# Summing four quarters of channels before the bias product, two of the three sums as accumulating DMA transfers

## The chip, the cores and the metric

The kernel runs on one NeuronCore of a Trainium2 chip. The core has a matrix engine (TensorE, PE in the profile), a vector engine (DVE), an activation engine (ACT), a general engine (GpSimd, POOL) and SyncE (SP), which here only starts transfers. Each works through its own queue in order; semaphores hold an instruction back until what it needs is there. Sixteen DMA engines move data. The metric is the device time of one execution in microseconds (us), as the median of several runs. The profile belongs to one execution.

## The reference, cut to what matters

The network has four layers on a small image. The change touches layer 0, a deformable attention block, and in it only the position bias. For each of 16 combinations of batch and head there are 1024 queries and 64 sampled keys. The bias of every query-key pair comes from a small network with 128 hidden channels in both of its layers:

```python
pos = grid_q[:, :, None, :] - grid_kv[:, None, :, :]
bias = jnp.sign(pos) * jnp.log1p(jnp.abs(pos))
bias = jax.nn.relu(bias @ cpb_w1 + cpb_b1)      # 2 -> 128
bias = jax.nn.relu(bias @ cpb_w2 + cpb_b2)      # 128 -> 128
bias = (bias @ cpb_w3 + cpb_b3)                 # 128 -> 1
sim = jnp.einsum('bhid,bhjd->bhij', qh, kh) + bias
attn = jax.nn.softmax(sim, axis=-1)
```

With 16 x 1024 x 64 query-key pairs the second line with a `relu` is by far the largest product of the layer. The last product sums 128 channels with the weights `cpb_w3`.

## The kernel before

Layer 0 works through a list `quads` of (u, o, jj): 16 values of u (batch and head), 8 of o, 2 of jj, 256 in all. One such step handles four keys (keys 32 jj + 4 o to 32 jj + 4 o + 3 of head u) for all 1024 queries. Two steps with jj = 0 and 1 form a pair.

**First hidden layer** (`first_hidden`, L392). DVE makes four tiles of 128 channels x 1024 queries, one for each key, from a table in SBUF and a row in PSUM, always one step ahead of their use. There are four `h1` buffers of two keys each.

**Second hidden layer** (`second_hidden`, L414). The 128 output channels are cut into four quarters q of 32. For each q, TensorE multiplies 32 columns of the weights with each of the four keys' tiles. The results stand side by side in one accumulator `hp`: partitions 32 k to 32 k + 31 hold key k. Three accumulators rotate. ACT then adds the bias and applies the `relu` (L418), writing a tile `y` of 128 x 1024 into the pool `hid2`.

**Last product by signs.** The absolute value of `cpb_w3` has been multiplied into the second layer's weights and bias ahead of time (`last_weights`), so the last product only has to add channels with a sign of plus or minus one. Before that product, quarters 0 and 1 are summed, and quarters 2 and 3: the even quarter is multiplied by the product of the two signs (`flip`; on ACT at L425 for q = 0, on POOL at L422 for q = 2), then POOL adds the odd quarter (L426). What is left is two tiles for each step.

**The last product** (`last_product`, L441). A matrix `ends` with the odd quarters' signs in a block pattern sums the 32 rows of each key and puts the result into the right row of the accumulator `sim`. It runs once for a pair, with four products of 512 columns for each of the two sums.

**The order of the work** is written out by hand: the program order is the order in each queue of PE, ACT, DVE and POOL (`manual_schedule`). In a step the next step's first hidden layer is issued first, then this step's second one. The last product of a pair follows the second hidden layer of the next step (the jj = 0 step of the next pair). Behind each step come one piece of `after` (softmax and output of a finished head, `attend`, and at the end of a batch `projection`) and one piece of `front` (offsets and samples of the next channel tile, `offsets` and `sampled`). Loads of the tables `lb` go through SP's queue; no transfer is started by POOL.

After layer 0 come the block's own multi-layer perceptron and the three other layers, which the change leaves alone.

Of the kernel before, what the change touches and what calls it, by code (L numbers as in the profile page):

```python
# [11 lines left out]
F32 = mybir.dt.float32  # L12
AF = mybir.ActivationFunctionType
ALU = mybir.AluOpType
# [33 lines left out]
class Net:  # L48
# [50 lines left out]
    def layer0(self):  # L99


        nc, io = self.nc, self.io
        with ExitStack() as ctx:
            keep = self.pool(ctx, "l0")
            self.l0qkv = keep.tile([P, 3, CT, P], F32, tag="qkv", name="qkv")
            nc.scalar.dma_start(self.l0qkv, io["l0_qkv"])
            self.l0w2 = keep.tile([P, P], F32, tag="w2", name="w2")
            nc.scalar.dma_start(self.l0w2, io["cpb_w2"])
            ow = keep.tile([P, CT, C], F32, tag="ow", name="ow")
            nc.scalar.dma_start(ow, io["out_w"])  # L110
            self.s1 = self.bn(keep, "bn1")
            self.last_weights(keep)

            self.dram = ctx.enter_context(self.tc.tile_pool(name="l0_d", bufs=2, space=bass.MemoryType.DRAM))
            self.fpool = self.pool(ctx, "f", 2)
            self.fone = self.pool(ctx, "f1", 1)
            self.lpool = self.pool(ctx, "c_log", 2)
            self.tab = self.pool(ctx, "c_tab", 2)
            self.hid = self.pool(ctx, "c_hid", 4)
            self.hid2 = self.pool(ctx, "c_hid2", 11)  # L120
            self.soft = self.pool(ctx, "c_soft", 1)
            apool = self.pool(ctx, "c_att", 1)
            ps = self.ps_h = self.pool(ctx, "c_ps_h", 3, psum=True)

            self.bank = self.pool(ctx, "c_ps_t", 1, psum=True).tile([P, HF], F32, tag="bank", name="bank")
            ps_s = self.pool(ctx, "c_ps_s", 1, psum=True)

            engines = {getattr(mybir.EngineType, e) for e in ("PE", "Activation", "DVE", "Pool")}
            with self.tc.manual_schedule(engines=engines):
                pairs = [{} for _ in range(BP)]  # L130
                for _ in self.offsets(pairs[0], 0, ps):
                    pass
                front = [self.sampled(pairs[0], 0, ps)]
                after, sims, att = [], {}, None
                tables = {}
                quads = [(u, o, jj) for u in range(2 * BP) for o in range(8) for jj in range(2)]
                ready = self.first_hidden(*quads[0], pairs, tables)
                held = None
                for i, (u, o, jj) in enumerate(quads):
                    if o == 0 and jj == 0 and u % 2 == 0 and u // 2 + 1 < BP:  # L140
                        nxt = pairs[u // 2 + 1]
                        front += [self.offsets(nxt, u // 2 + 1, ps), self.sampled(nxt, u // 2 + 1, ps)]
                    h1 = ready
                    if i + 1 < len(quads):
                        if quads[i + 1][1:] == (7, 0) and u + 1 < 2 * BP:
                            self.advance(front, lambda: "logs" in pairs[(u + 1) // 2])
                        ready = self.first_hidden(*quads[i + 1], pairs, tables)
                    z = self.second_hidden(u, o, jj, h1)
                    if jj == 0:
                        if held is not None:  # L150
                            self.last_product(*held, sims, ps_s)
                            if held[1] == 7:
                                v = held[0]
                                if v % 8 == 0:
                                    self.advance(after, lambda: False)
                                    att = [
                                        apool.tile([P, N], F32, tag=f"att{t}", name=f"att{v}_{t}") for t in range(CT)
                                    ]
                                self.advance(front, lambda: "v" in pairs[v // 2])
                                after.append(self.attend(v, pairs[v // 2], sims.pop(v), att, ps))  # L160
                                if v % 8 == 7:
                                    after.append(self.projection(ps, att, ow, v // 8))
                        first = z
                    else:
                        held = (u, o, (first, z))
                    self.step(after)
                    self.step(front)
                self.last_product(*held, sims, ps_s)
                after.append(self.attend(u, pairs[u // 2], sims.pop(u), att, ps))
                self.advance(after, lambda: False)  # L170
                self.project(ps, att, ow, "out_b", B - 1)

    def last_weights(self, keep):

        nc = self.nc
        row = keep.tile([P, P], F32, tag="row", name="w3row")
        nc.scalar.dma_start(row, self.io["cpb_w3"].partition_broadcast(P))  # L180
        nc.vector.scalar_tensor_tensor(row, row, -1.0, row, ALU.mult, ALU.max)
        nc.vector.tensor_tensor(self.l0w2, self.l0w2, row, ALU.mult)
        w3 = self.colr("w3r", 4)
        self.magb = keep.tile([P, 4], F32, tag="magb", name="magb")
        nc.vector.scalar_tensor_tensor(self.magb, w3, -1.0, w3, ALU.mult, ALU.max)
        nc.vector.tensor_tensor(self.magb, self.magb, self.colr("b2r", 4), ALU.mult)
        sign = keep.tile([P, 4], F32, tag="sign", name="sign")
        nc.vector.tensor_scalar(sign, w3, 0.0, 2.0, ALU.is_ge, ALU.mult)
        nc.vector.tensor_scalar(sign, sign, -1.0, None, ALU.add)
        self.flip = keep.tile([P, 2], F32, tag="flip", name="flip")  # L190
        self.ends = keep.tile([P, 2, 60], F32, tag="ends", name="ends")
        nc.vector.memset(self.ends, 0.0)
        for p in range(2):
            nc.vector.tensor_tensor(
                self.flip[:, p : p + 1], sign[:, 2 * p : 2 * p + 1], sign[:, 2 * p + 1 : 2 * p + 2], ALU.mult
            )
            for k in range(4):
                rows = slice(32 * k, 32 * k + 32)
                nc.vector.tensor_copy(self.ends[rows, p, 28 + k : 29 + k], sign[rows, 2 * p + 1 : 2 * p + 2])

    @staticmethod
    def step(behind):
# [200 lines left out]
    def second_hidden(self, u, o, jj, h1):  # L403


        nc = self.nc
        got, before = [], None
        for q in range(4):
            hp = self.ps_h.tile([P, N], F32, tag="ps", name=f"hp_{u}_{o}{jj}{q}")
            for h in range(2):  # L410
                cut = slice(h * HF, (h + 1) * HF)
                for k in range(4):
                    rows = slice(32 * k, 32 * k + 32)
                    nc.tensor.matmul(  # L414
                        hp[rows, cut], lhsT=self.l0w2[:, 32 * q : 32 * q + 32], rhs=h1[k][:, cut], start=True, stop=True
                    )
            y = self.hid2.tile([P, N], F32, tag="h2", name=f"h2_{u}_{o}{jj}{q}")
            nc.scalar.activation(y, hp, AF.Relu, bias=self.magb[:, q : q + 1])  # L418
            if q % 2 == 0:
                before = y  # L420
                if q == 2:
                    nc.gpsimd.tensor_scalar(y, y, self.flip[:, 1:2], 1.0, ALU.mult, ALU.mult)  # L422
            else:
                if q == 1:
                    nc.scalar.activation(before, before, AF.Copy, scale=self.flip[:, 0:1])  # L425
                nc.gpsimd.tensor_tensor(y, y, before, ALU.add)  # L426
                got.append(y)
        return got

    def last_product(self, u, o, z, sims, ps_s):  # L430

# [2 lines left out]
        nc = self.nc  # L434
        if o == 0:
            sims[u] = ps_s.tile([P, HF], F32, tag="sim", name=f"sim{u}")
        for p in range(2):
            for h in range(2):
                for jj in range(2):
                    at = h * NJ + jj * 32  # L440
                    nc.tensor.matmul(  # L441
                        sims[u][at : at + 32, :],
                        lhsT=self.ends[:, p, 28 - 4 * o : 60 - 4 * o],
                        rhs=z[jj][p][:, h * HF : (h + 1) * HF],
                        start=(o == 0 and p == 0),
                        stop=False,
                    )

    def attend(self, u, m, sim, att, ps):
        nc = self.nc  # L450
# [701 lines left out]
```

## Time and profile before

| | us |
|---|---|
| median of 3 runs | 3705.47 (3703.88 to 3705.98) |
| span of the profiled execution | 3703.5 |
| layer 0's hidden matmuls, first to last start | 42.2 to 2186.3 |
| PE busy, of the span | 3610.2 (97%) |
| POOL, ACT busy, of the span | 1868.3 and 1860.3 (50% each) |
| POOL adds of quarters (L426), 512 | 1228.7 |
| sim matmuls (L441), 2048 recorded | 251.1 |

Two things help in reading it. A float32 matmul appears as two recorded instructions, so the 8 matmuls of one `last_product` are 16 in the trace. And an instruction's mean time is not its cost where several run beside each other: the matmuls of 32 columns work in groups of four, so the distance between groups is what counts. Idle time of an engine names who released it; on an engine that doesn't set the pace, that idle time costs nothing.

### The profile page before, as it was taken

How to read it: one execution, taken by the hardware profiler on the slowest of the kernel's cores; microseconds unless marked ns; L12 is line 12 of the kernel's file. 1: busy time of each engine (PE TensorE's matmuls, PEld its weight loads, DVE VectorE, ACT ScalarE, POOL GpSimd, SP SyncE). 2: the span in 40 equal slices, each digit the busy share in tenths (PEclk: the TensorE clock that was granted, in tenths of full speed). 3: DMA queues.
4: the chain of work that ended last, by engine and by line, in shares of the span. 5: the costliest groups of instructions: out<-in, count | busy, mean ns of one | idle time of the engine just before them, and what ended most of it. 6: DMA issues, size and time to landing. Idle time of an engine off the chain costs nothing.

```text
span 3703.5 us, 59657 instructions
## 1 busy us (share of the span) xinstructions
PE 3610.2 (97%) x26176; PEld 1282.8 (35%) x26176; DVE 2036.4 (55%) x2075; ACT 1860.3 (50%) x1873; POOL 1868.3 (50%) x1013
## 2 busy tenths in 40 slices
PE   5999999999999999999999989999989999999998
PEld 2232332332333332332333324444454333343333
DVE  5777667668667567668666640000052377522764
ACT  4766676776766576766667641100010266102661
POOL 3777777777776577777777750000001244012441
PEclk8999999999999999999999999999999999999999
DMA  3000000000000000000100021000000000000001
GB/s 91 16 18 18 17 21 13 20 18 20 13 18 18 14 18 16 17 18 20 34 14 22 15 91 46 0 0 0 0 4 1 35 1 1 16 0 1 1 1 47
DMA packets 28628, 68.37 MB, mean 18 GB/s; under 512 B 4416, under 2 KB 6080, under 8 KB 27072
## 3 DMA queue, kind: packets, MB, share of 16 engines
q1 hardware_dynamic: 27488, 62.34, 5.9%
q8 instruction: 209, 3.42, 0.4%
q10 hardware_dynamic: 864, 2.06, 0.2%
q14 instruction: 67, 0.55, 0.1%
HBM read 59.92 MB, written 4.46 MB: 17 GB/s over the span
## 4 chain that ended last, share of the span: by engine, by line
PE 88%; DVE 10%; DMA 1%; issue 1%; POOL 0%; ACT 0%; DVEq 0%; ACTq 0%; SPq 0%; POOLq 0%
PE hp L414 42%; PE m L545 6%; PE m L554 6%; PE s L882 6%; PE o L911 6%; PE sim L441 5%; DVE h L392 4%; PE qk0p L774 3%; PE pb L511 3%; PE qk1p L774 3%; PE vp L815 3%; DVE prod L245 2%; PE out_b L511 2%; DVE conv L258 1%; PE d L928 1%
## 5 line engine op out<-in xcount | busy, mean ns | idle before, releaser
L414 PE MATMUL hp<-h,w 128*32 128x512 f32 x16384 | 1822.2, 593 | 16.6 <-DVE h L392 15.0
L426 POOL TENSOR_TENSOR h<-h,h 128x1024 f32<-128x1024 f32 x512 | 1228.7, 2400 | 576.4 <-ACT h L425 555.0
L418 ACT ACTIVATE h<-hp,magb 128x1024 f32<-128x1024 f32 x1024 | 1139.0, 1112 | 659.0 <-PE hp L414 621.8
L392 DVE CUSTOM_DVE_ANT_1 h<-tx,bank 128x1024 f32<-128x1024 f32 x1024 | 1180.5, 1216 | 393.3 <-PE hp L414 386.2
L414 PEld LDWEIGHTS hp<-h,w 128*32 128x32 f32 x16384 | 530.1, 110 | 1246.5 <-issue 1196.4
L886 ACT ACTIVATE e<-s 128x1024 f32<-128x1024 f32 x256 | 258.6, 1023 | 152.8 <-PE s L882 152.7
L422 POOL TENSOR_SCALAR h<-h,flip 128x1024 f32<-128x1024 f32 x256 | 297.5, 1162 | 0.0
L425 ACT ACTIVATE h<-h,flip 128x1024 f32<-128x1024 f32 x256 | 291.0, 1137 | 0.0
L882 PE MATMUL s<-q,k 64*64 64x512 f32 x2048 | 259.9, 590 | 5.1 <-ACT e L886 3.4
L911 PE MATMUL o<-e,v 64*64 64x512 f32 x2048 | 260.8, 592 | 0.0
L441 PE MATMUL sim<-h,ends 128*32 128x512 f32 x2048 | 251.1, 594 | 2.9 <-POOL h L426 2.9
L585 POOL MEMSET l1ones<- 128x128 f32 x1 | 0.2, 204 | 483.8 <-PE m L554 483.8
L545 PE MATMUL m<-mx,w 128*128 128x512 f32 x512 | 220.5, 592 | 0.8 <-DVE x L515 0.8
L554 PE MATMUL m<-mh,w 128*128 128x512 f32 x512 | 220.4, 592 | 0.0
L549 ACT ACTIVATE mh<-m,cols 128x512 f32<-128x512 f32 x64 | 44.0, 687 | 336.5 <-PE m L545 336.5
L893 POOL TENSOR_TENSOR some<-some,e 128x1024 f32<-128x1024 f32 x64 | 151.2, 2363 | 82.6 <-ACT e L886 80.2
L562 DVE SCALAR_TENSOR_TENSOR x<-m,cols,x 128x512 f32<-128x512 f32 x16 | 12.0, 751 | 318.0 <-PE m L554 318.0
L891 POOL TENSOR_TENSOR some<-e,e 128x1024 f32<-128x1024 f32 x32 | 75.8, 2369 | 212.6 <-ACT q L920 139.2
L788 POOL TENSOR_TENSOR sq<-q 128x1024 f32<-128x1024 f32 x16 | 30.3, 1892 | 279.3 <-DVE q L782 279.3
L786 ACT ACTIVATE k<-qk1p,cols 128x512 f32<-128x512 f32 x32 | 22.0, 687 | 244.5 <-PE qk1p L774 244.5
L545 PEld LDWEIGHTS m<-mx,w 128*128 128x128 f32 x512 | 97.2, 190 | 123.6 <-issue 122.0
L554 PEld LDWEIGHTS m<-mh,w 128*128 128x128 f32 x512 | 97.3, 190 | 122.4 <-issue 122.4
(180 smaller groups left out, 2420.6 us busy)
## 6 DMA issues: line engine op xcount, KB each, us to landing
lb<-logs SPq DMA_DIRECT2D x64, 512.0 KB, 4.9
w<-in_mlp_w SPq DMA_DIRECT2D x8, 1024.0 KB, 12.1
qkv<-in_l_qkv SPq DMA_DIRECT2D x8, 768.0 KB, 6.4
x<-in_x SPq DMA_DIRECT2D x8, 512.0 KB, 8.1
out<-x SPq DMA_DIRECT2D x8, 512.0 KB, 2.6
proj<-in_l_proj SPq DMA_DIRECT2D x8, 256.0 KB, 5.9
l1w<-in_l_w SPq DMA_DIRECT2D x1, 1280.0 KB, 6.9
ow<-in_out_w ACTq DMA_DIRECT2D x1, 1024.0 KB, 12.2
```

The costliest lines, as they stand in the source:

```text
L392: self.nc.vector._custom_dve(TENSOR_ADD_SAT, out=h[:, k, :, :], in0=x[:, jj, 2 * r + k, :].unsqueeze(1).to_broadcast([P, H, W]), in1=y[:, ...
L414: nc.tensor.matmul(hp[rows, cut], lhsT=self.l0w2[:, 32 * q : 32 * q + 32], rhs=h1[k][:, cut], start=True, stop=True)
L418: nc.scalar.activation(y, hp, AF.Relu, bias=self.magb[:, q : q + 1])
L422: nc.gpsimd.tensor_scalar(y, y, self.flip[:, 1:2], 1.0, ALU.mult, ALU.mult)
L425: nc.scalar.activation(before, before, AF.Copy, scale=self.flip[:, 0:1])
L426: nc.gpsimd.tensor_tensor(y, y, before, ALU.add)
L441: nc.tensor.matmul(sims[u][at : at + 32, :], lhsT=self.ends[:, p, 28 - 4 * o : 60 - 4 * o], rhs=z[jj][p][:, h * HF : (h + 1) * HF], start= ...
L545: nc.tensor.matmul(acc, lhsT=w1[t][:, o * P : (o + 1) * P], rhs=xn[t], start=(t == 0), stop=(t == CT - 1))
L554: nc.tensor.matmul(acc, lhsT=w2[t // 4][:, t % 4, o * P : (o + 1) * P], rhs=hs[t], start=(t == 0), stop=(t == nh - 1),)
L882: nc.tensor.matmul(s[halves[c], par, :], lhsT=ks[p][rows, at : at + DH], rhs=qs[p][rows, cut], start=True, stop=True)
L886: nc.scalar.activation(e, s, AF.Exp)
L911: nc.tensor.matmul(o[halves[par], r, :], lhsT=v[rows, n, at : at + DH], rhs=e[rows, par, :], start=(n == 0), stop=(n == NB - 1),)
```

## The change

All four quarters are summed before the last product, so that one tile for each step is left and `last_product` runs four products for a pair instead of eight. Each of the first three quarters is multiplied by its sign times the sign of quarter 3. Quarter 0 is flipped by ACT, quarter 1 by ACT in jj = 0 steps and by POOL in jj = 1 steps, quarter 2 by POOL.

Of the three sums one stays an add on POOL (quarter 3 += quarter 2). The other two are transfers inside SBUF that add to their destination: quarter 1 += quarter 0 is started in the step itself, and quarter 3 += quarter 1 (`join`) in the following step, right after that step's own first transfer. Both go through POOL's queue.

The last product of a pair is issued one step later than before, after the second hidden layer of the next pair's jj = 1 step. The eleven buffers of `hid2` become 2, 3, 2 and 4 for the four quarters.

```diff
-            self.hid2 = self.pool(ctx, "c_hid2", 11)
+            self.hid2 = self.pool(ctx, "c_hid2", 1)
...
                     z = self.second_hidden(u, o, jj, h1)
                     if jj == 0:
+                        first = z
+                    else:
                         if held is not None:
                             self.last_product(*held, sims, ps_s)
...
-                        first = z
-                    else:
                         held = (u, o, (first, z))
...
+                self.join()
                 self.last_product(*held, sims, ps_s)
...
-            y = self.hid2.tile([P, N], F32, tag="h2", name=f"h2_{u}_{o}{jj}{q}")
+            y = self.hid2.tile([P, N], F32, tag=f"h2{q}", bufs=(2, 3, 2, 4)[q], name=f"h2_{u}_{o}{jj}{q}")
+            ys.append(y)
             nc.scalar.activation(y, hp, AF.Relu, bias=self.magb[:, q : q + 1])
-            if q % 2 == 0:
-                before = y
-                if q == 2:
+            if q == 1:
+                nc.scalar.activation(ys[0], ys[0], AF.Copy, scale=self.flip[:, 0:1])
+                if jj == 1:
                     nc.gpsimd.tensor_scalar(y, y, self.flip[:, 1:2], 1.0, ALU.mult, ALU.mult)
-            else:
-                if q == 1:
-                    nc.scalar.activation(before, before, AF.Copy, scale=self.flip[:, 0:1])
-                nc.gpsimd.tensor_tensor(y, y, before, ALU.add)
-                got.append(y)
-        return got
+                else:
+                    nc.scalar.activation(y, y, AF.Copy, scale=self.flip[:, 1:2])
+                nc.gpsimd.dma_start(y, ys[0], accum_op=ALU.add)
+                if self.join:
+                    self.join()
+            elif q == 2:
+                nc.gpsimd.tensor_scalar(y, y, self.flip[:, 2:3], 1.0, ALU.mult, ALU.mult)
+            elif q == 3:
+                nc.gpsimd.tensor_tensor(y, y, ys[2], ALU.add)
+        self.join = lambda: nc.gpsimd.dma_start(ys[3], ys[1], accum_op=ALU.add)
+        return ys[3]
...
-        for p in range(2):
-            for h in range(2):
-                for jj in range(2):
-                    at = h * NJ + jj * 32
-                    nc.tensor.matmul(
-                        sims[u][at : at + 32, :],
-                        lhsT=self.ends[:, p, 28 - 4 * o : 60 - 4 * o],
-                        rhs=z[jj][p][:, h * HF : (h + 1) * HF],
-                        start=(o == 0 and p == 0),
-                        stop=False,
-                    )
+        for h in range(2):
+            for jj in range(2):
+                at = h * NJ + jj * 32
+                nc.tensor.matmul(
+                    sims[u][at : at + 32, :],
+                    lhsT=self.ends[:, 28 - 4 * o : 60 - 4 * o],
+                    rhs=z[jj][:, h * HF : (h + 1) * HF],
+                    start=(o == 0),
+                    stop=False,
+                )
```

More of the change, by code (lines that the diff above doesn't have):

```diff
@@ L137, in layer0 @@
                 ready = self.first_hidden(*quads[0], pairs, tables)
-                held = None
+                held, self.join = None, None
                 for i, (u, o, jj) in enumerate(quads):
@@ L189, in last_weights @@
         nc.vector.tensor_scalar(sign, sign, -1.0, None, ALU.add)
-        self.flip = keep.tile([P, 2], F32, tag="flip", name="flip")
-        self.ends = keep.tile([P, 2, 60], F32, tag="ends", name="ends")
+        self.flip = keep.tile([P, 3], F32, tag="flip", name="flip")
+        nc.vector.tensor_tensor(self.flip, sign[:, 0:3], sign[:, 3:4].to_broadcast([P, 3]), ALU.mult)
+        self.ends = keep.tile([P, 60], F32, tag="ends", name="ends")
         nc.vector.memset(self.ends, 0.0)
-        for p in range(2):
-            nc.vector.tensor_tensor(
-                self.flip[:, p : p + 1], sign[:, 2 * p : 2 * p + 1], sign[:, 2 * p + 1 : 2 * p + 2], ALU.mult
-            )
-            for k in range(4):
-                rows = slice(32 * k, 32 * k + 32)
-                nc.vector.tensor_copy(self.ends[rows, p, 28 + k : 29 + k], sign[rows, 2 * p + 1 : 2 * p + 2])
+        for k in range(4):
+            rows = slice(32 * k, 32 * k + 32)
+            nc.vector.tensor_copy(self.ends[rows, 28 + k : 29 + k], sign[rows, 3:4])
     @staticmethod
@@ L406, in second_hidden @@
         nc = self.nc
-        got, before = [], None
+        ys = []
         for q in range(4):
@@ L436, in last_product @@
             sims[u] = ps_s.tile([P, HF], F32, tag="sim", name=f"sim{u}")
-        for p in range(2):
-            for h in range(2):
-                for jj in range(2):
-                    at = h * NJ + jj * 32
-                    nc.tensor.matmul(
-                        sims[u][at : at + 32, :],
-                        lhsT=self.ends[:, p, 28 - 4 * o : 60 - 4 * o],
-                        rhs=z[jj][p][:, h * HF : (h + 1) * HF],
-                        start=(o == 0 and p == 0),
-                        stop=False,
-                    )
+        for h in range(2):
[8 more added lines that the diff above has]
+                )
     def attend(self, u, m, sim, att, ps):
```

## The prediction

> **What bounds the kernel now.** I read the page first: busy time, then the costliest groups. After that came the chain of work in order of time, the timeline of one pair of calls inside layer 0, and the DMA table. A "call" is one run of `second_hidden`; a "pair" is the two calls (jj = 0, then 1) that share one `last_product`. There are 256 calls and 128 pairs, all between 42 and 2193 us.
>
> ```profile
> PE 3610.2 (97%) x26176; PEld 1282.8 (35%) x26176; DVE 2036.4 (55%) x2075; ACT 1860.3 (50%) x1873; POOL 1868.3 (50%) x1013
> ...
> L414 PE MATMUL hp<-h,w 128*32 128x512 f32 x16384 | 1822.2, 593 | 16.6 <-DVE h L392 15.0
> L426 POOL TENSOR_TENSOR h<-h,h 128x1024 f32<-128x1024 f32 x512 | 1228.7, 2400 | 576.4 <-ACT h L425 555.0
> L418 ACT ACTIVATE h<-hp,magb 128x1024 f32<-128x1024 f32 x1024 | 1139.0, 1112 | 659.0 <-PE hp L414 621.8
> ...
> L422 POOL TENSOR_SCALAR h<-h,flip 128x1024 f32<-128x1024 f32 x256 | 297.5, 1162 | 0.0
> L425 ACT ACTIVATE h<-h,flip 128x1024 f32<-128x1024 f32 x256 | 291.0, 1137 | 0.0
> ...
> L441 PE MATMUL sim<-h,ends 128*32 128x512 f32 x2048 | 251.1, 594 | 2.9 <-POOL h L426 2.9
> ```
>
> TensorE is idle 16.6 us before all 16384 recorded hidden-layer matmuls, while ACT and POOL each idle some 600 us waiting for something upstream. So PE sets the pace. The mean of 593 ns is one instruction's latency, not its cost, as four run beside each other. The chain gives the cost:
>
> ```profile
> 256.70 1.72 PE sim L441 x16
> 258.42 13.73 PE hp L414 x128
> 272.15 1.72 PE sim L441 x16
> 273.87 13.73 PE hp L414 x128
> 287.60 1.72 PE sim L441 x16
> 289.32 13.73 PE hp L414 x128
> ```
>
> A pair is 15.45 us: 128 hidden instructions in 13.73 us and 16 sim instructions in 1.72 us, each 0.43 us per group of four. Nothing else is on the chain in such a stretch. Where ACT and POOL stand in the pair that begins at 273.69:
>
> ```profile
> 278.45 1.14 ACT L425 ACTIVATE h<-h,flip 128x1024 f32<-128x1024 f32 x1
> ...
> 279.66 2.38 POOL L426 TENSOR_TENSOR h<-h,h 128x1024 f32<-128x1024 f32 x1 [2.69 <-ACT h L425]
> ...
> 286.47 2.38 POOL L426 TENSOR_TENSOR h<-h,h 128x1024 f32<-128x1024 f32 x1 [0.85 <-ACT h L425]
> ...
> 287.42 1.90 PE L441 MATMUL sim<-h,ends 128*32 128x512 f32 x16
> ```
>
> POOL starts a call's first add 0.07 us after the flip, 5.97 us into the jj = 0 call.
>
> Not all of the stage looks like that. Once in each of the seven later channel tiles the chain moves to DVE for about 46 us (321 to 367 is the first), about three pairs, because the offsets, the sampling and the softmax are queued there between the first-hidden operations. Two lines from that stretch:
>
> ```profile
> 345.32 2.38 DVE L480 TENSOR_TENSOR e<-e,st 128x512 f32<-128x512 f32 x1
> ...
> 347.62 5.26 DVE L245 TENSOR_TENSOR prod<-qpad,cols 128x384 f32<-128x384 f32 x3
> ```
>
> The same `prod` instruction takes 0.815 us at its shortest, so three of them lose 2.8 us here to something that isn't their own work.
>
> **What the skill says.** (1) The Trainium skill, "DMA: Bandwidth & Descriptors", section on the anatomy of one DMA on the gpsimd path: such a transfer costs about 2.0 us fixed plus bytes over 436 GB/s. The trace before has no DMA issued by POOL. Its SP-issued ones agree on the rate and come in lower on the fixed part:
>
> ```profile
> 2197.00:2199.00 2.00, 0.00 (x0) 0.00 (x0) 2.00 (x5) 0.24 (x1) 0.00 (x0) 0.89 1.02 430
> ...
> lb<-logs SPq DMA_DIRECT2D x64, 512.0 KB, 4.9
> ...
> out<-x SPq DMA_DIRECT2D x8, 512.0 KB, 2.6
> ```
>
> The last columns of the window line are the share of the DMA engines and GB/s: 430 at full use. A 512 KB store lands 2.6 us after issue; 524288 bytes at 430 GB/s are 1.22 us, so 1.4 us are fixed. (2) "Collectives: The Full Stack", section on the bandwidth ceiling: a reducing transfer costs about twice a copy since it reads two sources, not because of the add. No run here shows that. (3) "SBUF — State Buffer", section on who interferes with whom: a DVE instruction with two SBUF inputs and a GpSimd instruction that reads SBUF lock each other out. The stretched `prod` and `e` lines agree.
>
> **The change part by part.**
>
> *PE, removed.* `last_product` issues 8 recorded sim instructions for a pair instead of 16: two groups of four, 2 x 0.429 = 0.86 us. The floor of a pair falls from 15.45 to 14.59 us. In the DVE-bound stretches (7 x 3 = 21 pairs) a shorter PE buys nothing. That leaves 107 x 0.86 = 92 us.
>
> *POOL.* Before, a pair holds 4 adds at 2.39 and 2 flips at 1.16, 11.9 us; with half a `tx` (64 of about 0.8 us over 128 pairs) 12.3. After: 2 adds, 3 flips (q = 2 in both calls, q = 1 at jj = 1) and half a `tx` are 8.66 us, plus four DMA issues of D each. D isn't in the trace. Below: 0.36 us, which the SP queue's issue of `lb` takes. Above: the whole 2.0 us fixed part. I take 1.0, half of it: 12.7 us in 14.6, so POOL still waits for ACT. POOL becomes the bound at D = (14.59 - 8.66)/4 = 1.48.
>
> *ACT.* 8 relus at 1.112 and 3 flips at 1.137 make 12.3 us of 14.6 (was 11.2 of 15.45), so ACT keeps up on average. With two flips after q = 1 of a jj = 0 call, the q = 2 relu starts at 6.94 instead of 5.80 and q = 3 ends near 9.2. PE has three accumulators and wants q = 2's at 6.86 + 1.72 = 8.6 or later; the relu is done at 8.05. Nothing, then, with 0.5 us to spare. ACT's table loads (1.28 us) fall in the gap after jj = 1.
>
> *The new wait.* `last_product` now waits for the landing of the second DMA (`join`) of the pair's jj = 1 call, which POOL issues during the next jj = 0 call, after that call's own first DMA. Counted from that call's start, both flips end at 6.94 and POOL begins the first issue at 7.0. PE reaches the sim matmuls at 13.73. Behind that wait on PE stand all the following hidden matmuls. Let L run from 7.0 to the landing; it has 6.7 us. Moving costs 2 x 1.22 = 2.44 us for one accumulate by (2), and the second queues behind the first: 4.88 us. With the trace's 1.4 us fixed L = 6.3; with the skill's 2.0 it is 6.9. Bounds: 2 x 1.22 + 1.4 = 3.8, if an accumulate moves like a copy; 2 x 3.66 + 2.0 = 9.3, if its two reads and its write follow each other at 430 GB/s. I take 6.6, which just fits; as half of the spread is over, I allow 0.1 us for a pair, 10 us in all.
>
> *The other waits.* POOL's `join` waits for a DMA issued a call earlier, about 8 us before, so it has landed. ACT's relu of q = 0 waits until the first DMA of two calls before has read its source: issued by 9, landed near 13, wanted after 14.6. Q = 1 (3 buffers) and q = 3 (4) have more time.
>
> *DVE in its stretches.* The six `prod` (4.51 + 5.26 - 6 x 0.815) and `e` (2.38 against 0.69 for its like before) lose 6.6 us to the lock in such a stretch. POOL's reading operations fall from 11.9 of 15.45 (77%) to 8.3 of 14.6 (57%), which would give back a quarter, 1.7 x 7 = 12 us. It could also be nothing, as lock waits depend on phase; I count half, 6 us.
>
> *The end of the stage.* Before, the last relu ends at 2188.14 and the last add lets PE go at 2191.7. After, the same add is followed by a DMA of about 4.4 us: plus 3 us, once.
>
> *At nothing.* The smaller `ends` and `flip` set-up lies under the load of `w3row`, which the chain shows to 17 us. SP's queue is unchanged; its `lb` loads take 1.2 us of the DMA engines once in two pairs, 4%.
>
> *Sum against this span, 3703.5:* -92 - 6 + 10 + 3 = -85, 3618. Runs stand 2 us above the span: **3620**. Without any stall and with the whole gain in all 128 pairs it would be 3703.5 - 110 = 3594.
>
> **The rivals.**
>
> *The landing decides (chance 0.17, slower).* A pair then takes 7.0 + L + 0.86. It breaks even with 15.45 at L = 7.6 and loses 1 us for each further one. At L = 9.1 a pair is 16.96: 107 x 1.51 = +162, 3865; at L = 8.2 it is +65, 3770. For it: two serial transfers in a slot that they nearly fill, with a rate nobody has measured here. Against it: 430 GB/s at full use, and a rate that reads and writes at once.
>
> *POOL becomes the bound by issuing (0.12, slower).* From D = 1.7 a pair is longer than before: 8.66 + 6.8 = 15.46. At D = 2.0 it is 16.7, and 107 x 1.2 = +130, 3834. For it: an accumulate needs two read descriptors for one write. Against it: 2.0 holds the landing as well.
>
> *A part is eaten (0.13, faster).* L between 6.9 and 7.5, or D of 1.5 to 1.65: 0.2 to 0.8 us of a pair go, 107 of them, 21 to 86 us over the 3608 without a stall: 3630 to 3694.
>
> *Nothing moves (0.03).* The same with all of it gone. That the change doesn't do what it says is hardly possible: halving the sim instructions is in the order of instructions.
>
> **How the numbers follow.** The main case has 0.55 and a range of its own of 3590 to 3640. A difference of 0.2%, about 7 us, is what a measurement of this kernel can tell from no change. Faster 0.55 + 0.13 = 0.68; same 0.03; slower 0.29. Low end: 3590, the full gain and a little lock relief. For the high end, the slower cases start at 3713 and centre near 3770 to 3850; 3800 leaves about 0.15 above and 0.05 below.
>
> **What would show it.** The sim group at half its count and about 126 us; on the chain, pairs of 14.6 us (13.73 + 0.86). POOL's DMA issues of about 1 us each, landing some 4 us after issue. Wrong: `sim` waiting for a DMA on PE in every pair (the landing), or POOL without waits for ACT (issue cost), or ACT's relus waiting for a DMA (buffers). `prod` still near 1.6 us on the mean would refute the lock's part.

## The result and the profile after

| | us |
|---|---|
| before, median | 3705.64 (3703.88 to 3705.98) |
| after, median | 3762.37 (3760.06 to 3774.32) |
| ratio after to before, 95% interval | 1.0161 (1.0139 to 1.0183) |
| span of the profiled execution after | 3758.9 |

The change made the kernel 57 us slower. The forecast was 3620 us; the result lies on the other side, in the part of the range that was kept open for the slower cases.

These are the page's lines after, for the groups shown of before (busy us, mean ns of one, idle time before it and what ended most of that):

```profile
PE 3579.0 (95%) x25152; PEld 1393.5 (37%) x25152; DVE 2055.7 (55%) x2070; ACT 1972.0 (52%) x2001; POOL 1864.5 (50%) x1397
...
q0 software_dynamic: 73728, 268.47, 37.8%
...
L413 PE MATMUL hp<-h,w 128*32 128x512 f32 x16384 | 1891.9, 593 | 25.5 <-DVE h L390 18.1
...
L431 POOL TENSOR_TENSOR h<-h,h 128x1024 f32<-128x1024 f32 x256 | 614.8, 2402 | 21.4
L425 POOL DMA_DIRECT2D h<-h x256 | 225.0, 879 | 547.6 <-ACT h L424 493.3
L429 POOL TENSOR_SCALAR h<-h,flip 128x1024 f32<-128x1024 f32 x256 | 448.8, 1753 | 0.0
...
L445 PE MATMUL sim<-h,ends 128*32 128x512 f32 x1024 | 229.2, 603 | 82.7 <-DMA h<-h 82.5
L432 POOL DMA_DIRECT2D h<-h x256 | 299.7, 1171 | 1.6 <-issue 1.3
...
h<-h POOLq DMA_DIRECT2D x512, 512.0 KB, 6.5
```

The last product has half its instructions, as planned. Yet its busy time fell only from 251.1 to 229.2, because waiting tears its groups of four apart, and it now has an idle time of 82.7 us that a transfer ends. POOL still waits 493 us for ACT ahead of its first transfer (L425), so POOL's issuing isn't the bound. The last line says that a transfer lands 6.5 us after its issue; that is the median of two kinds. The views of the two lines, the first transfer of a step (L425) and then `join` (L432), keep them apart:

```profile
DMA to landing us min/median/max: 4.6/4.7/8.1
```

```profile
DMA to landing us min/median/max: 4.6/7.1/10.0
```

One pair in the timeline shows the wait. These are PE's and POOL's lines of one stretch (start us, duration, what, in brackets the idle time before it and who ended it):

```profile
280.30 0.63 PE L445 MATMUL sim<-h,ends 128*32 128x512 f32 x3 [1.72 <-DMA h<-h]
...
280.85 13.82 PE L413 MATMUL hp<-h,w 128*32 128x512 f32 x124
...
288.34 0.88 POOL L425 DMA_DIRECT2D h<-h  x1 [4.49 <-ACT h L424]
288.93 1.17 POOL L432 DMA_DIRECT2D h<-h  x1
...
291.34 2.39 POOL L431 TENSOR_TENSOR h<-h,h 128x1024 f32<-128x1024 f32 x1
...
294.27 0.59 PE L445 MATMUL sim<-h,ends 128*32 128x512 f32 x1
...
296.94 0.63 PE L445 MATMUL sim<-h,ends 128*32 128x512 f32 x3 [1.65 <-DMA h<-h]
```

The hidden matmuls of the pair begin at 280.85 and PE is through with them 13.7 us later. It runs the products of the jj = 0 half, which is there, and stands still for the jj = 1 half until 296.94. The pair before was released at 280.30, so a pair lasts 16.6 us where it lasted 15.45.

The DMA engines in the same stretch, in slices of half a microsecond (the last two columns are the share of the engines and GB/s):

```profile
289.00:289.50 0.50, 0.50 (x11) 0.29 (x8) 0.50 (x2) 0.50 (x2) 0.50 (x2) 1.00 0.00 0
289.50:290.00 0.50, 0.50 (x11) 0.26 (x5) 0.50 (x1) 0.50 (x1) 0.50 (x2) 1.00 0.72 131
...
291.00:291.50 0.50, 0.50 (x11) 0.25 (x7) 0.50 (x1) 0.12 (x1) 0.42 (x2) 1.00 1.06 197
...
294.50:295.00 0.50, 0.50 (x8) 0.00 (x0) 0.00 (x0) 0.37 (x1) 0.50 (x1) 1.00 0.83 156
295.00:295.50 0.50, 0.29 (x4) 0.00 (x0) 0.38 (x1) 0.32 (x1) 0.50 (x1) 1.00 0.08 8
295.50:296.00 0.50, 0.00 (x0) 0.00 (x0) 0.50 (x1) 0.50 (x1) 0.20 (x2) 1.00 0.08 16
296.00:296.50 0.50, 0.00 (x0) 0.00 (x0) 0.50 (x2) 0.29 (x1) 0.50 (x2) 1.00 0.04 8
```

In quarter slices the engines stand idle until 289.75. The first packets go at about 289.8, 1.4 us after the first issue. Fifteen of the sixteen engines are through with both transfers at about 295.1: 5.3 us for 1.05 MB, about 200 GB/s with the engines fully busy. One engine is not. It is what the last two slices still show, 0.08 of the engines at work: it moves the last packets of the second transfer until 296.6, and PE is released 0.3 us later. So the landing comes 8.6 us after the first issue (288.34 to 296.94): about 1.4 to the first packets, 5.3 of movement, 1.5 for the one engine and 0.3 to the release. The DMA view of this stretch (288.34 to 296.94) has one packet of another queue in it, the one that the page calls instruction:

```profile
q0 software_dynamic: 288, 1.05, 64.9%
q8 instruction: 1, 0.02, 0.7%
```

In the packet records it has 16 KB, starts at 293.66 and takes 0.97 us. One engine carries it between its packets of the second transfer, where each of those takes about 0.33 us.

A landing without such a packet looks different. These are lines of the same two engines later on:

```profile
827.93 0.63 PE L445 MATMUL sim<-h,ends 128*32 128x512 f32 x3 [0.27 <-DMA h<-h]
...
835.97 0.88 POOL L425 DMA_DIRECT2D h<-h  x1 [2.98 <-ACT h L424]
...
843.16 0.63 PE L445 MATMUL sim<-h,ends 128*32 128x512 f32 x3 [0.23 <-DMA h<-h]
```

Here PE is released 7.2 us after the first issue, and the pair lasts 15.23 us, a little less than before. Over all 127 pairs whose landing can be read this way, the landing comes 7.15 us after the first issue in the median of the 38 pairs in which no packet of another queue (instructions, or loads such as those of the tables `lb`) falls among the two transfers' own. In 56 pairs it takes 8.4 us or more, and each of those 56 has such a packet. On them fall 62 of the 76 us that PE's products wait for a transfer in these pairs. The trace of experiment 7 shows the same, 7.15 in 39 pairs and all 52 long landings with such packets. No run took the other packets away, so this is read from traces and not shown by an experiment.

### The profile page after: what moved, and what is told of

Read it like the earlier page. It is cut to its first block, busy times and chain, and to the rows that moved or that the text cites. A ratio compares the mean times of both kernels' runs of the same rounds, so it can differ in the third digit from the quotient of the medians.

```text
span 3758.9 us, 58788 instructions
## 1 busy us (share of the span) xinstructions
PE 3579.0 (95%) x25152; PEld 1393.5 (37%) x25152; DVE 2055.7 (55%) x2070; ACT 1972.0 (52%) x2001; POOL 1864.5 (50%) x1397
## 3 DMA queue, kind: packets, MB, share of 16 engines
q0 software_dynamic: 73728, 268.47, 37.8%
## 4 chain that ended last, share of the span: by engine, by line
PE 57%; POOL 15%; issue 12%; DMA 7%; DVE 6%; ACT 3%; POOLq 0%; ACTq 0%; SPq 0%; DVEq 0%
PE hp L413 15%; DMA h<-h 6%; POOL h L431 6%; PE m L549 6%; PE m L558 6%; PE s L886 6%; PE o L915 6%; PE pb L515 3%; PE qk0p L778 3%; PE qk1p L778 3%; POOL h L425 3%; PE vp L819 3%; POOL h L432 2%; ACT h L418 2%; DVE h L390 2%
## 5 line engine op out<-in xcount | busy, mean ns | idle before, releaser
L413 PE MATMUL hp<-h,w 128*32 128x512 f32 x16384 | 1891.9, 593 | 25.5 <-DVE h L390 18.1
L418 ACT ACTIVATE h<-hp,magb 128x1024 f32<-128x1024 f32 x1024 | 1120.3, 1111 | 586.3 <-PE hp L413 586.3
L413 PEld LDWEIGHTS hp<-h,w 128*32 128x32 f32 x16384 | 668.8, 110 | 1130.6 <-issue 905.9
L431 POOL TENSOR_TENSOR h<-h,h 128x1024 f32<-128x1024 f32 x256 | 614.8, 2402 | 21.4
L425 POOL DMA_DIRECT2D h<-h x256 | 225.0, 879 | 547.6 <-ACT h L424 493.3
L429 POOL TENSOR_SCALAR h<-h,flip 128x1024 f32<-128x1024 f32 x256 | 448.8, 1753 | 0.0
L445 PE MATMUL sim<-h,ends 128*32 128x512 f32 x1024 | 229.2, 603 | 82.7 <-DMA h<-h 82.5
L432 POOL DMA_DIRECT2D h<-h x256 | 299.7, 1171 | 1.6 <-issue 1.3
L897 POOL TENSOR_TENSOR some<-some,e 128x1024 f32<-128x1024 f32 x64 | 151.2, 2363 | 82.7 <-ACT e L890 80.3
L422 POOL TENSOR_SCALAR h<-h,flip 128x1024 f32<-128x1024 f32 x128 | 152.3, 1190 | 30.6 <-ACT h L418 30.6
```

Source lines behind the costliest of these rows:

```text
L413: nc.tensor.matmul(hp[rows, cut], lhsT=self.l0w2[:, 32 * q : 32 * q + 32], rhs=h1[k][:, cut], start=True, stop=True)
L425: nc.gpsimd.dma_start(y, ys[0], accum_op=ALU.add)
L429: nc.gpsimd.tensor_scalar(y, y, self.flip[:, 2:3], 1.0, ALU.mult, ALU.mult)
L431: nc.gpsimd.tensor_tensor(y, y, ys[2], ALU.add)
L432: self.join = lambda: nc.gpsimd.dma_start(ys[3], ys[1], accum_op=ALU.add)
```

## The experiments

**1. A product that waits for no transfer.** The second transfer adds into a spare tile. All transfers and their places in the queue stay.

```diff
-        self.join = lambda: nc.gpsimd.dma_start(ys[3], ys[1], accum_op=ALU.add)
+        self.join = lambda: nc.gpsimd.dma_start(self.scratch(), ys[1], accum_op=ALU.add)
...
```

(`scratch` hands out two zeroed spare tiles in turn.)

> The changed kernel, but the second transfer (join) adds quarter 1 into one of two spare tiles instead of into quarter 3; every transfer, its size and its place in POOL's queue stay, and the last product waits for POOL's add alone. Left out: quarters 0 and 1 are missing from the bias. Theory A (the landing of the second transfer, on which the last product waits, is the whole of the loss): no PE wait for a DMA at the sim matmuls, a pair of 14.6 us instead of 16.7, time 3610 to 3640. Rival B (POOL's issuing, ACT's extra flip or the 268 MB moved beside the matmuls slow the pair, and the wait only shows it): pair stays above 15.5, time 3700 or more.

Measured: 3635.7 us, ratio to before 0.9811 (0.9796 to 0.9826). PE's lines show pairs of 14.59 us without a wait:

```profile
266.50 13.92 PE L416 MATMUL hp<-h,w 128*32 128x512 f32 x128
280.23 1.04 PE L452 MATMUL sim<-h,ends 128*32 128x512 f32 x8
281.09 13.92 PE L416 MATMUL hp<-h,w 128*32 128x512 f32 x128
```

The wait alone turned a gain into a loss: with the same 268 MB moved, the same work on POOL and ACT and the product in the same place, this kernel is 127 us faster than the change and 71 faster than before. Rival B falls.

**2. The same sums, the product one step later.** Now it follows the jj = 0 step of the pair after next, so the landing has a whole step more.

```diff
-                held, self.join = None, None
+                held, self.join = [], None
...
                     if jj == 0:
                         first = z
-                    else:
-                        if held is not None:
-                            self.last_product(*held, sims, ps_s)
...
+                        if len(held) == 2:
+                            done = held.pop(0)
+                            self.last_product(*done, sims, ps_s)
...
-            y = self.hid2.tile([P, N], F32, tag=f"h2{q}", bufs=(2, 3, 2, 4)[q], name=f"h2_{u}_{o}{jj}{q}")
+            y = self.hid2.tile([P, N], F32, tag=f"h2{q}", bufs=(2, 3, 2, 5)[q], name=f"h2_{u}_{o}{jj}{q}")
...
-        qp = m["q"] = self.fpool.tile([P, HP, HP], F32, tag="qpad", name=f"qpad{b}{t}")
+        qp = m["q"] = self.fpool.tile([P, HP, HP], F32, tag="qpad", bufs=3, name=f"qpad{b}{t}")
```

> The changed kernel with the last product one step later still (after the jj = 0 step of the pair after next), for which quarter 3 gets 5 buffers instead of 4 and the padded query tile 3 instead of 2. Same sums, same transfers. Theory A: the landing has a whole step more (7 us), it came 2.4 us late, so the wait is gone: pair 14.6, time 3610 to 3640, faster than both kernels. Rival B: as before, above 3700. Rival C (the transfers themselves are the bound, so that the backlog grows however late the product is): still 16.7 for a pair and the same wait, about 3760.

Measured: 3616.2 us (3615.2 to 3618.2), ratio to before 0.9757 (0.9744 to 0.9770). With all the sums of the change it is faster than both kernels: 90 us less than before, 146 less than the change. PE's timeline in its undisturbed stretch:

```profile
261.89 13.92 PE L415 MATMUL hp<-h,w 128*32 128x512 f32 x128
275.62 1.04 PE L447 MATMUL sim<-h,ends 128*32 128x512 f32 x8
276.48 13.92 PE L415 MATMUL hp<-h,w 128*32 128x512 f32 x128
290.22 1.04 PE L447 MATMUL sim<-h,ends 128*32 128x512 f32 x8
```

A pair is 14.59 us from 261.89 to 276.48, the floor that the prediction worked out. The transfers still land a median of 6.5 us after issue; in this stretch nobody waits for them. Rival C falls too.

**3. Half the columns.** Both transfers move 512 of 1024 columns.

```diff
-                nc.gpsimd.dma_start(y, ys[0], accum_op=ALU.add)
+                nc.gpsimd.dma_start(y[:, 0:HF], ys[0][:, 0:HF], accum_op=ALU.add)
```

(and the same for `join`)

> The changed kernel with both transfers cut to the first 512 of 1024 columns (2 KB in a partition instead of 4). Left out: the sums of quarter 0 and 1 for the other half of the queries. Theory A with bytes as the cost: each transfer moves in 1.3 us instead of 2.65, so the second lands 2.65 us sooner, 13.4 us into the pair where PE arrives at 13.7: pair 14.6 to 14.8, time 3610 to 3650. If the fixed parts (start and completion) or the number of packets carry the cost: the landing hardly moves, pair above 16, time above 3730.

Measured: 3646.7 us in one run. The chain in order of time has undisturbed pairs of 14.59:

```profile
267.69 13.73 PE hp L413 x128
281.42 0.86 PE sim L445 x8
282.28 13.73 PE hp L413 x128
```

The number of transfers and of packets (73728) is the same, so bytes carry most of the moving cost. The queue's share of 21.5% over 3644.8 us makes 1.53 us for one transfer, against 2.77 (37.8% of 3758.9 us over 512) for the whole.

**4. Copies in place of adding transfers.**

```diff
-                nc.gpsimd.dma_start(y, ys[0], accum_op=ALU.add)
+                nc.gpsimd.dma_start(y, ys[0])
```

(and the same for `join`)

> The changed kernel with both transfers as plain copies in place of adding ones, the same 512 KB from the same queue. Left out: the adding, so that quarter 0 overwrites quarter 1, and that overwrites quarter 3. If adding costs a second read of the same size: a copy moves in about 1.3 us, the second lands near 13.4, pair 14.6 to 14.8, time 3610 to 3650. If POOL-issued transfers move at 200 GB/s whatever they do: 2.65 us each as before, pair 16.7, time about 3760.

Measured: 3642.5 us in one run. The page's queue table and DMA issues:

```profile
q0 software_dynamic: 73728, 268.47, 18.6%
...
h<-h POOLq DMA_DIRECT2D x512, 512.0 KB, 3.7
```

And one half-microsecond slice with the engines full (share and GB/s at the end):

```profile
290.50:291.00 0.50, 0.50 (x11) 0.25 (x7) 0.50 (x1) 0.50 (x2) 0.50 (x1) 1.00 1.00 410
```

The same bytes from the same queue move at 410 GB/s and take 1.32 us for one transfer (18.6% of 3640.7 over 512). Adding makes it 2.1 times as long. With copies the landing falls to 3.7 us and the wait nearly vanishes (PE idle 8.1 us ahead of sim).

**5. Three quarters of the columns**, as a dose between 3 and the change.

> The changed kernel with both transfers cut to 768 of 1024 columns. Left out: the sums of quarter 0 and 1 for the last quarter of the queries. This is a dose between the half (a transfer moves in 1.53 us, pair 14.59) and the whole (2.77 us, pair 16.7). Theory A says that a pair is the landing plus 0.86 as soon as the landing is later than 13.73: a transfer of 2.15 us puts it 1.24 us ahead of the whole, so pair 15.4 to 15.6, about the pair of the kernel before, and time about 3690 to 3705. A rival in which the wait is a matter of some threshold, for example the two transfers colliding with others, would leave it at 14.6 or at 16.7.

Measured: 3697.1 us in one run. The releases in PE's timeline:

```profile
257.54 0.63 PE L445 MATMUL sim<-h,ends 128*32 128x512 f32 x3 [0.53 <-DMA h<-h]
...
273.12 0.63 PE L445 MATMUL sim<-h,ends 128*32 128x512 f32 x3 [0.60 <-DMA h<-h]
...
288.62 0.63 PE L445 MATMUL sim<-h,ends 128*32 128x512 f32 x3 [0.52 <-DMA h<-h]
```

Pairs of 15.58 and 15.50 us, as expected, with a transfer of 2.16 us (29.9% of 3695.2 over 512). From here to the change the two transfers take 1.2 us more and the pair 1.1 more: once the landing is later than PE, it sets the pair about one for one.

**6. The join first, then the step's own transfer.** The two issues change places.

> The changed kernel with the order of the two issues in a step exchanged: join first, then the step's own transfer. Same sums, same buffers. Simple form of theory A: the join no longer queues behind another transfer, so it lands 2.7 us sooner, PE doesn't wait, pair 14.6, time 3610 to 3650. Full form of A: join waits on POOL for the landing of the transfer before it, the step's own transfer is issued 0.6 us later and moves behind it, and lands 1.25 + 2 x 2.65 + 2.0 = 8.6 us after that; so every step takes about 9.1 us on a chain from landing to issue, pair 18, time 3850 to 3950, with POOL waiting for a DMA.

Measured: 3793.9 us in one run, 31 us more than the change. POOL's timeline:

```profile
278.40 0.87 POOL L432 DMA_DIRECT2D h<-h  x1 [2.32 <-DMA h<-h]
...
286.09 0.88 POOL L432 DMA_DIRECT2D h<-h  x1 [1.21 <-DMA h<-h]
...
295.68 0.88 POOL L432 DMA_DIRECT2D h<-h  x1 [4.18 <-DMA h<-h]
```

POOL, for which the change's trace records no wait for these transfers, now waits 512.6 us for them over 206 issues, and all behind it in its queue waits too. The full form had the sign and the place right, but a step takes 7.7 to 9.6 us here, not 9.1 each time, so the size was too large. The first step in these lines is the undisturbed 7.15 us from issue to landing and half a microsecond to the next issue; the expectation had counted a delayed landing in every step. Issuing a transfer sooner doesn't help when its input is the landing of the one before.

**7. Three buffers for the padded query tile**, the other difference in experiment 2.

> The changed kernel with 3 buffers instead of 2 for the padded query tile, the only other difference between the changed kernel and the run with the later product. Theory A: POOL's waits for that tile (30.8 us in 6 places) are gone; each holds back POOL's next transfers, so some 10 to 30 us less than the changed kernel, 3730 to 3752, and the pair stays at 16.7. If these waits were the real cause: near 3620.

Measured: 3765.3 us, ratio to before 1.0159 (1.0142 to 1.0176), the change's own. The expected 10 to 30 us didn't come, though POOL's waits for that tile are gone from the trace; probably they lay beside PE's wait for the landing. So the gain of experiment 2 over the change belongs to the later product with its fifth buffer for quarter 3. The fifth buffer was not tried alone, but in the change ACT's relus wait for no buffer: the page has all of their idle time, 586.3 us, down to PE.

**8. Why the free product (1) was 20 us above the later one (2).** First the same tile buffers:

> The first experiment (second transfer into a spare tile, one instead of two here, so that the last product waits for no transfer; quarters 0 and 1 missing from the bias) with 3 buffers for the padded query tile. It stood at 3635.7, the later product with 3 buffers at 3616.2. If POOL's and ACT's waits for that tile (18.9 and 16.5 us in the first experiment, 0 and 5.2 in the later one) are the 20 us between them: 3612 to 3622. If the 20 us are due to the place of the product in PE's order: unchanged, 3632 to 3640.

Measured: 3632.1 us, ratio 0.9803 (0.9787 to 0.9820). Only 4 us less, but this run doesn't settle it: it has one spare tile where experiment 1 has two, and POOL waits 84.2 us for it, in 64 places. Then, with two buffers and two spare tiles again, the place of the product, put back to where it stood before the change:

> The first experiment (second transfer into a spare tile, so that the last product waits for no transfer; quarters 0 and 1 missing from the bias) with the last product one step earlier, after the jj = 0 step, where the kernel before has it. If the 16 to 20 us between the runs with a free product (3635.7 and 3632.1) and the one with the later product (3616.2) come from the step that the product follows (after jj = 0, where ACT does two flips, its 0.86 us of PE give ACT time, and PE waits 31 us for ACT instead of 56): 3612 to 3622. If they come from something else in the spare-tile runs, such as their transfers: 3630 to 3640.

Measured: 3591.2 us (3587.5 to 3593.8), ratio 0.9688 (0.9672 to 0.9705). The place decides, and by more than expected: 44 us less than in experiment 1, from which it differs by the place alone. What hidden matmuls (weight loads and products together) waited for ACT's relus, from the view of that line, first for experiment 1, then for experiment 2, then for this last one (us, times):

```profile
  ACT h L421: 55.8, 155
```

```profile
  ACT h L420: 31.0, 96
```

```profile
  ACT h L421: 24.1, 83
```

In the jj = 0 step ACT does two flips; a product behind that step gives ACT 0.86 us more to free an accumulator. The trace agrees in the place: at the matmuls of quarter 0 in jj = 1 steps these waits are 20.7 us in experiment 1, 4.7 in experiment 2 and 3.9 here. The waits for DVE went the same way: 90.2, 75.8 and 50.8. Both have the order of the three times. Why DVE's shrink, too, isn't shown. Of the 25 us between experiments 2 and this one, about 6 are the end of the stage (from PE's first sim matmul behind the last hidden one to the first transpose 14.1 against 8.5 us); the rest stands beside 25 us less waiting for DVE, and its cause is open.

## Why the prediction was wrong, step by step

**The step that failed is L,** the landing of the second transfer after POOL begins the first. The prediction put it at 6.6, with 6.7 us to spend. It is 7.15 where nothing else moves and 8.4 to 10.4 in 56 of 127 pairs.

- *What was mis-sized:* two moves of 2.65 each instead of 2.44, +0.4. The fixed part is about 1.8 (1.4 to the first packets, some 0.4 from the last to PE's release), against the 1.7 that 6.6 contains; it held. A first transfer of a step alone lands after 4.6 us when undisturbed, 2.0 more than its 2.65 of moving. So the fixed 2.0 us of the Trainium skill, "DMA: Bandwidth & Descriptors", section on the anatomy of one DMA, agrees with this trace.
- *What was put at nothing:* other transfers on the same engines. The prediction counted the `lb` loads as 4% of the engines' time and instruction packets not at all. That is right for the average, but PE is released by the last of the sixteen engines, and an engine that carries such a packet ends later: 1.5 us in the pair shown above.
- *What POOL added:* it begins 7.5 us into the pair, not 7.0. About half comes from the start, 0.30 us after ACT's flip where an add started 0.07 after it, the other half from a relu of quarter 1 that stands 4.0 us into the pair, not 3.74. That leaves 6.2 us, not 6.7.

By the undisturbed landing a pair takes 15.2 us, 0.2 less than before: the rival "a part is eaten". The loss comes with the long landings.

**The mechanism was the first rival,** with a chance of 0.17: a pair of 7.0 + L + 0.86. With 7.5 and 8.6 it gives 16.96; measured 16.6 to 16.7, as half of the product, the jj = 0 half, runs ahead of the wait. From release to release that is 0.55 to the next hidden matmuls, 7.49 to POOL's first issue and 8.60 to the landing. Its price was too high, though. It let all 107 pairs pay and came to 3865 for a pair of 16.96. PE's products waited for a transfer 68 times (its weight loads 96 times) in 128 pairs. In the others the landing came without the delay, or the projections, samples and DVE's stretches had already given it its time.

**What held.** The gain of PE, 0.86 us a pair and a floor of 14.59, was measured in experiments 2 and 3. The prediction's sum was -95 us on the span without its 10 us for waiting; experiment 2 has -89. In part that is luck: its hidden matmuls wait 31.0 us for ACT's relus and 75.8 for DVE (2.0 and 56.7 before). For ACT's the prediction had counted nothing. POOL's issue cost of 1.0 is about right: from the first issue at 288.34 to the add at 291.34 are 3.0 us, less 1.16 for the flip between, 0.92 for each. ACT kept up in the undisturbed stretch. Outside it the prediction put nothing on ACT; with the wait away, the place of the product alone is worth 44 us (experiment 1 against the last), part of it waits for ACT. That an accumulate costs two moves of a copy held: 2.77 against 1.32 us.

**What is mixed.** The lock between DVE and POOL: the 42 `prod` took 1518 ns on the mean after, 1580 before, 2.5 us in all, so by its own sign (`prod` still near 1.6) that part hardly moved. But the 16 `e` of the same kind fell from 23.4 to 14.8 us. Together that is 11 us of DVE's time, where the prediction counted 6; how much of it reached PE isn't shown.

**What didn't.** The end of the stage: from the last relu to the last release of the sim matmuls are 9.1 us (3.6 before), 2.5 more than the 3 added for it.

**Where the choice went wrong.** The prediction knew both ends, 3.8 and 9.3, and that 6.7 was the limit. It then took a value 0.1 us below the limit and gave this case 0.55. Even the undisturbed 7.15 is beyond that limit. With a slot in the middle of an unmeasured range the two sides should have had equal chances.

## What to carry to other kernels

A sum moved from an engine to a transfer must be read by its landing, not by its issue or its bytes: work out the time from issue to release, two chained transfers in one queue as one number, and place the consumer behind it with more room than the uncertainty of that number. An average share of other traffic says nothing of the last engine: here a few packets of other queues made 8.6 us out of 7.15. Where the slot is short, a consumer one step later and one more buffer settle it (3616 against 3762 us here); issuing sooner can make it worse, because a transfer that waits for another's landing holds up everything behind it in its queue. And where two places in the order are equal for the data, try the one behind the step that loads the engine which frees the accumulators; here the choice was worth 44 us.

## What the runs showed of the hardware that was not expected

- A 512 KB transfer inside SBUF that adds to its destination moves at about 200 GB/s with the DMA engines fully busy (2.77 us), a copy from the same queue at about 410 (1.32 us). With 256, 384 and 512 KB the adding one took 1.53, 2.16 and 2.77 us.
- Two adding transfers in a row land 7.15 us after the first issue when the engines are theirs: 1.4 ahead of the first packets, 5.3 of movement, some 0.4 to the release. A transfer lands with the last of its sixteen engines: with one 16 KB instruction packet of 0.97 us on one engine it was 8.6.
- The pressure of 268 MB beside the matmuls cost PE nothing that shows: where PE didn't wait, 128 hidden instructions stayed at 13.92 us (13.73 from start to start), 0.43 for a group of four.
